# Last-slot products in pairs on half the rows, the last silu one round earlier, and sums stored by partition, in the tail of an attention and expert block

## The chip, the cores and the metric

The kernel runs on one core of a Trainium2 chip. The metric is the device time of one execution in microseconds (us). Engines are named as in the profile: PE is TensorE (PEld its weight loads), DVE VectorE, ACT ScalarE, POOL GpSimd, SP SyncE; SPq and ACTq are the DMAs that SP and ACT issue.

## What is computed

The input is x of 16 x 256 x 256 in float32. Two steps follow each other, each with its residual:

```
x = x + layernorm(attention(layernorm(x)))      # 16 heads of 128, weights as codes times scales
x = x + layernorm(ffn(layernorm(x)))

# ffn, tokens T = 4096, width 256, experts E = 64, K = 6 per token, capacity C = 96
pos  = sum(cumsum(onehot) * onehot) - 1          # place of a token in its expert's list
slot = expert * C + min(pos, C - 1)              # all that come too late share the last slot
out  = (silu(buf @ Wg.T) * (buf @ Wu.T)) @ Wd.T  # buf: the token in each slot
y    = sum over k of out[slot[t, k]] * weight[t, k]
ffn  = y + (silu(x @ Sg.T) * (x @ Su.T)) @ Sd.T  # one shared expert for all tokens
```

Each expert's last slot can serve many tokens, so its result has to be added to every token that overflowed, with that token's weight.

## The kernel before

The tokens are 32 chunks of 128 (NC = 32, P = 128), in 8 groups of 4 chunks (CG = 4). The first stage is attention and the routing. The second, `ffn`, is what the change is about, with some lines in the first that prepare for it.

**Experts.** The loop of L958 goes over 64 experts, 96 slots each. Each result is scaled by its token's weight (L909) and added by an indirect DMA of POOL (L910) to one of three arrays in HBM, `y_ds[0..2]` (from expert 44 on only the first two), at the row that the token's number says. That number travels with the token: `toki` (L127), copied into the row of `h` (L457), comes out as `toks` (L866). Three arrays are used so that an addition has not to wait for the one just before it. They are cleared in the first stage (`clear_sums`, L250), and for groups 0 to 3 the shared expert's result is what `y_ds[0]` begins with (`shared_put`, L770, L780). Row t of these arrays belongs to token t. The result of each expert's last slot is collected, row by row, into `ol`, of 64 x 256 (L917).

**Overflow.** In routing, each token's weights for last slots are set out as a 64 x 4096 array in HBM, `ovT_d` (L616). A group of tokens gets its last-slot contributions as a product of 64 rows: `ovT` of 64 x 128 (one chunk) times `ol` of 64 x 256.

**The tail.** The end of `ffn` (L997 to L1101) works through the 8 groups in the order `ends = [0, 5, 1, 2, 6, 3, 4, 7]` (L921). All of it is inside `tc.manual_schedule()`, so each engine runs its instructions in the order in which the code issues them. A round n, with g = ends[n], has these steps:

- `put_out(n, c)` (L997), for c = 0 and c = 2: PE makes the last-slot products of two chunks into one PSUM tile, ahead of them, for groups 5, 6 and 7, the last product of the shared expert (`shared_out`, L761, three products of up to 128 rows per chunk). The tile of c = 0 is from pool `ps`, that of c = 2 from `pso`; each pool has two buffers, so that round n can't begin to write before round n - 2 has been read. DVE adds the tile to the group's sum (L1008).
- `shared_in(*pieces[n])` (L1073): PE begins the shared expert's gate and up products for a later group, one third of its width at a time.
- `norm(n - 1, ...)` (L1035): DVE takes a reciprocal and a product (L1039, L1041), POOL another (L1042), and ACT scales the four chunks of the group before (L1045).
- `sum_y(n + 1)` (L1010): POOL adds up the sums that were loaded from HBM.
- POOL issues the addition of group n - 1 into the output, which holds the residual (L1082).
- DVE's two adds; `take_stats` (L1016): for some rounds another addition (L1021), then mean and variance of four chunks.
- `shared_act(*act)` (L1090): ACT's silu and DVE's product for the piece that the round before began.
- `take_root` (L1029): ACT's square root, L1032.

The last round leaves this loop at L1085 and does its adds, statistics and roots for two halves of the group, c = 0 and 2 (L1093), then the factors, the scaling and the residual (from `xl`) for both halves, and writes each half out by SP (L1101). Of the shared pieces, `pieces` (L922) says in which round each begins: (7, 2), the last one, in round 4, and so its silu comes in round 5:

```
if act:
    shared_act(*act)
act = pieces.get(n)
take_root(n, 0, CG)
```

The sums of the tail are loaded by SP: `load_early` (L938) loads the third array's and the first six groups' `ovT` during the experts; `load_ov` and 16 `load_sum` (L1052, L1056) come after the experts.

Of the kernel before, what the change touches and what calls it, by code (L numbers as in the profile page):

```python
# [9 lines left out]
F32 = mybir.dt.float32  # L10
# [4 lines left out]
ALU = mybir.AluOpType  # L15
# [3 lines left out]
P = 128  # L19
B, S, D = 16, 256, 256  # L20
NH, HD = 16, 128
FEAT = NH * HD
T = B * S
NC = T // P
# [4 lines left out]
E, M, CAP, K = 64, 176, 96, 6  # L29
# [7 lines left out]
CG = 4  # L37
# [6 lines left out]
SG0 = NC // CG // 2  # L44
# [6 lines left out]
def block_kernel(ctx, tc, x, wq, sq, wk, sk, wv, sv, wo, so, bqk, bv, bo, gateT, wg, wu, wd, sgT, suT, sdT, out):  # L51
    nc = tc.nc
    x_v = x.rearrange("(c p) d -> p c d", p=P)
    out_v = out.rearrange("(c p) d -> p c d", p=P)
# [4 lines left out]
    ovT_d = dram.tile([E, T], F32, name="ovT_d")  # L59
    buf_d = dram.tile([E * CAP, RW], F32, name="buf_d")  # L60

    y_ds = [dram.tile([T, D], F32, name=f"y{i}_d") for i in range(NY)]

    keep = ctx.enter_context(tc.tile_pool(name="keep", bufs=1))
    lastt = keep.tile([P, E], F32, name="lastt")
# [31 lines left out]
    def attention(split):  # L97
# [25 lines left out]
        base = rc.tile([P, E], F32, name="base")  # L123
        nc.gpsimd.iota(base, [[CAP, E]], base=1, channel_multiplier=0, allow_small_or_imprecise_dtypes=True)
        tokid = rc.tile([P, NC], F32, name="tokid")
        nc.gpsimd.iota(tokid, [[P, NC]], base=0, channel_multiplier=1, allow_small_or_imprecise_dtypes=True)
        toki = rc.tile([P, NC], I32, name="toki")  # L127
        nc.gpsimd.iota(toki, [[P, NC]], base=0, channel_multiplier=1)
        far = rc.tile([P, 1], F32, name="far")
        nc.gpsimd.iota(far, [[0, 1]], base=8192, channel_multiplier=8192, allow_small_or_imprecise_dtypes=True)  # L130
        nc.vector.memset(lastt, 0.0)
# [14 lines left out]
        zero = cp.tile([P, 256], F32, name="zero")  # L146
# [103 lines left out]
        def clear_sums(i):  # L250
            with tc.issue_after(marks[-1].ins):
                nc.vector.memset(zero, 0.0)
            r0 = 0 if i else SG0 * CG * P
            n = (T - r0) // P
            nc.sync.dma_start(
                y_ds[i][r0:T].rearrange("(p r) d -> p r d", p=P), zero.unsqueeze(1).to_broadcast([P, n, D])
            )

        in_mv = cp.tile([P, NC, 2], F32, name="in_mv")
        in_rs = cp.tile([P, NC], F32, name="in_rs")  # L260
# [398 lines left out]
        n = len(steps)  # L659
# [51 lines left out]
    def ffn(nm_, last_route, ph0):  # L711
# [10 lines left out]
        last = cp.tile([CAP, 1], F32, name="last")  # L722
        nc.gpsimd.iota(last, [[0, 1]], base=0, channel_multiplier=1, allow_small_or_imprecise_dtypes=True)
        nc.vector.tensor_scalar(last, last, float(CAP - 1), None, ALU.is_equal)
        ol = cp.tile([E, D], F32, name="ol")

        sg_t = cp.tile([P, DC, MS], F32, name="sg_t")
        nc.sync.dma_start(sg_t, sgT.rearrange("(c p) m -> p c m", p=P))
# [23 lines left out]
        def shared_act(g, i):  # L752
            m = MS_CH[i][1]
            if i == 0:
                aTs[g] = ep.tile([P, len(MS_CH), CG * P], F32, tag="aT", name=f"aT{g}")
            pg, pu = gus.pop((g, i))
            sg = ep.tile([P, CG * P], F32, tag="ssg", name=f"ssg{g}_{i}")
            nc.scalar.activation(sg[0:m, :], pg[0:m, :], AF.Silu)
            nc.vector.tensor_mul(aTs[g][0:m, i, :], sg[0:m, :], pu[0:m, :])

        def shared_out(po, g, c, start, stop):  # L761
            for i, (m0, m) in enumerate(MS_CH):
                nc.tensor.matmul(
                    po, lhsT=aTs[g][0:m, i, c * P : (c + 1) * P], rhs=sd_t[0:m, i, :],
                    start=start and i == 0, stop=stop and i == len(MS_CH) - 1,
                )
# [3 lines left out]
        def shared_put(g, c):  # L770

            if c == 0:
                ss[g] = ep.tile([P, CG, D], F32, tag="ssg2", name=f"s{g}", bufs=1)
            s = ss[g]
            po = ps.tile([P, 2, D], F32, tag="o", name=f"so{g}_{c}")
            for i in range(2):
                shared_out(po[:, i, :], g, c + i, True, True)
            nc.scalar.copy(s[:, c : c + 2, :], po)
            if c and g < SG0:
                nc.scalar.dma_start(y_ds[0][g * CG * P : (g + 1) * CG * P].rearrange("(c p) d -> p c d", p=P), s)  # L780

        NG_ = E // EG
        wts, bns, bTs, wcs, toks, prods, acts, obs = {}, {}, {}, {}, {}, {}, {}, {}
# [137 lines left out]
        ends = [0, G, 1, 2, G + 1, 3, SG0, G + 2]  # L921
        pieces = {0: (G + 1, 1), 1: (G + 1, 2), 2: (G + 2, 0), 3: (G + 2, 1), 4: (G + 2, 2)}  # L922
        direct = (1, 3, 5)
        ys, ovTs, stat = {}, {}, {}
        Y, V = CG * D, CG * P

        def place(t, at, g, i):

            ys.setdefault(g, {})[i] = t[:, at : at + Y].rearrange("p (c d) -> p c d", d=D)

        def load_sum(g, i):
            nc.sync.dma_start(ys[g][i], y_ds[i][g * V : (g + 1) * V].rearrange("(c p) d -> p c d", p=P))

        def load_ov(t, at, g):
            ovTs[g] = t[0:E, at : at + V]
            nc.sync.dma_start(ovTs[g], ovT_d[:, g * V : (g + 1) * V])

        def load_early(k):  # L938

# [9 lines left out]
        with tc.manual_schedule():  # L949
# [8 lines left out]
            for e in range(E + 2):  # L958
                g, j = e // EG, e % EG
# [23 lines left out]
                g, j = divmod(e - 1, EG)  # L983
# [10 lines left out]
            yp = ph5.enter_context(tc.tile_pool(name="yp" + nm_, bufs=2, reuse_waits="tile"))  # L994
            pso = ph7.enter_context(tc.tile_pool(name="pso" + nm_, bufs=2, side="right", space=PSUM, reuse_waits="tile"))

            def put_out(n, c):  # L997

                g = ends[n]
                y = ys[g][0 if n in direct else 2][:, c : c + 2, :]  # L1000
                po = (pso if c else ps).tile([P, 2, D], F32, tag="o", name=f"ov{g}_{c}")
                for i in range(2):
                    if g > SG0:
                        shared_out(po[:, i, :], g, c + i, True, False)
                    nc.tensor.matmul(
                        po[:, i, :], lhsT=ovTs[g][:, (c + i) * P : (c + i + 1) * P], rhs=ol, start=g <= SG0, stop=True
                    )
                return lambda: nc.vector.tensor_tensor(y, y, po, ALU.add)  # L1008

            def sum_y(n):  # L1010
                y = ys[ends[n]]
# [17 lines left out]
            def take_root(n, c, m):  # L1029
                g = ends[n]  # L1030
                rs = yp.tile([P, m], F32, tag=f"rs{m}", name=f"rs{g}_{c}")
                nc.scalar.activation(rs, stat[g, c][:, :, 1], AF.Sqrt, bias=eps_t)  # L1032
                stat[g, c] = rs, stat[g, c]

            def norm(n, c, m, eng):  # L1035

                g = ends[n]
                rs, mv = stat.pop((g, c))
                nc.vector.reciprocal(rs, rs)  # L1039
                nb = yp.tile([P, m], F32, tag=f"nb{m}", name=f"nb{g}_{c}")  # L1040
                nc.vector.tensor_scalar(nb, rs, -1.0, None, ALU.mult)  # L1041
                eng.tensor_tensor(nb, nb, mv[:, :, 0], ALU.mult)  # L1042
                y = ys[g][0]
                for i in range(m):
                    nc.scalar.activation(  # L1045
                        y[:, c + i, :], y[:, c + i, :], AF.Identity, bias=nb[:, i : i + 1], scale=rs[:, i : i + 1]
                    )

            nt, last = len(ends), ends[-1]
            t = xp.tile([P, EG * RW], F32, tag="bn", name="yv", bufs=5)  # L1050
            for i, g in enumerate(ends[EWB:]):
                load_ov(t, i * V, g)  # L1052
            nc.gpsimd.tensor_add(ys[SG0][2], ys[SG0][2], ss[SG0])
            for g in ends:
                for i in range(2):
# [2 lines left out]
            t = xp.tile([P, EG * RW], F32, tag="bn", name="xl", bufs=5)  # L1058
            xl = t[:, 0:Y].rearrange("p (c d) -> p c d", d=D)
# [8 lines left out]
            sum_y(0)  # L1068
            act = (G + 1, 0)
            for n, g in enumerate(ends):  # L1070
                add = [put_out(n, 0), put_out(n, 2)]
                if n in pieces:
                    shared_in(*pieces[n])  # L1073

                if n:
                    norm(n - 1, 0, CG, nc.gpsimd)
                if n + 1 < nt:
                    sum_y(n + 1)
                if n:
                    h = ends[n - 1]  # L1080
                    behind_stored(
                        nc.gpsimd.dma_start(out_v[:, h * CG : (h + 1) * CG, :], ys[h][0], accum_op=ALU.add), h  # L1082
                    )
                if n + 1 == nt:
                    break  # L1085
                for f in add:
                    f()
                take_stats(n, 0, CG)
                if act:
                    shared_act(*act)  # L1090
                act = pieces.get(n)
                take_root(n, 0, CG)
            for f, c in zip(add, (0, 2)):  # L1093
                f()
                take_stats(n, c, 2)
                take_root(n, c, 2)
            for c, eng in ((0, nc.gpsimd), (2, nc.vector)):
                norm(n, c, 2, eng)
                y = ys[last][0][:, c : c + 2, :]
                eng.tensor_add(y, y, xl[:, c : c + 2, :])  # L1100
                nc.sync.dma_start(out_v[:, last * CG + c : last * CG + c + 2, :], y)  # L1101
            ph7.close()
            ph5.close()
            ph4.close()
# [3 lines left out]
    flag, r, ph0 = attention(True)  # L1108
# [46 lines left out]
```

## Time and profile before

| | us |
|---|---|
| median of 3 runs | 1474.4 (1471.49 to 1476.71) |
| the profiled execution, its own time | 1477.35 |
| its span in the profile | 1475.5 |
| PE busy | 1428.8 (97%) |
| DVE busy | 1108.1 (75%) |
| ACT busy | 670.8 (45%) |
| POOL busy | 370.2 (25%) |

The span is that of the records of one execution on the chip; the execution's own time is 1.85 us more. A row of the profile names the source line, the engine, the operation, what is written from what, and the tile's partitions x elements. Products of float32 are recorded as two PE records each. "Idle before" is the time for which the engine stood, and the arrow names what released it. A table by windows gives busy time and, in brackets, the number of instructions of each engine in a stretch of time, then the TensorE clock that was granted (1.00 is full), the mean busy share of the DMA engines, and GB/s.

### The profile page before, as it was taken

The numbers are of one execution on the slowest core, as the hardware profiler recorded it, in microseconds if no ns is written. First come the engines' busy times: TensorE is split into PE (matmuls) and PEld (weight loads), VectorE is DVE, ScalarE is ACT, GpSimd is POOL, SyncE is SP. The second block draws the span as 40 slices with busy tenths as digits, with TensorE's granted clock in tenths as the row PEclk, the third lists the DMA queues.
The fourth block names the chain that finished last, engine by engine and source line by source line (L and its number), as shares of the span: only waits on it lengthen the run. The fifth ranks groups of instructions, "written<-read, shape, count | busy, mean of one in ns | idle before, by whom it ended". The sixth has DMA issues, their size and how long they took to land. (4 is left out here: it accounts for less than half of the span.)

```text
span 1475.5 us, 24749 instructions
## 1 busy us (share of the span) xinstructions
PE 1428.8 (97%) x8476; PEld 1208.6 (82%) x8476; DVE 1108.1 (75%) x3489; ACT 670.8 (45%) x1800; POOL 370.2 (25%) x345
## 2 busy tenths in 40 slices
PE   7999999999999999999999999999999999999995
PEld 4689899898989898898989898988798568878653
DVE  5787898878898988989798989888987324434364
ACT  4553463445444545544454445455454322323253
POOL 2330000230041006001400420060243315544572
PEclk9899999999999999999999999999999999999996
DMA  5246140240011101101010001001013979999594
GB/s 169 74 128 182 58 143 16 76 138 30 1 43 34 44 16 32 44 30 28 25 54 15 26 29 51 8 9 38 12 54 96 284 206 225 258 254 226 106 248 70
DMA packets 102928, 132.08 MB, mean 90 GB/s; under 512 B 15290, under 2 KB 85216, under 8 KB 102266
## 3 DMA queue, kind: packets, MB, share of 16 engines
q1 hardware_dynamic: 70570, 93.44, 21.2%
q0 software_dynamic: 21872, 20.75, 7.2%
q10 hardware_dynamic: 10352, 16.22, 3.8%
q8 instruction: 70, 1.15, 0.3%
q14 instruction: 64, 0.52, 0.1%
HBM read 82.50 MB, written 70.19 MB: 103 GB/s over the span
## 5 line engine op out<-in xcount | busy, mean ns | idle before, releaser
L336 ACT ACTIVATE pe<-sc,nms 128x256 f32<-128x256 f32 x512 | 240.2, 475 | 207.1 <-DVE nms L332 144.4
L594 POOL DMA_INDIRECT buf_d<-h,si x192 | 189.7, 988 | 508.5 <-DVE si L591 430.0
L361 PE MATMUL po<-pT,v 128*128 128x256 f32 x1024 | 277.0, 383 | 3.3 <-DVE oT L365 2.1
L328 PE MATMUL sc<-qk 128*128 128x256 f32 x1024 | 268.3, 382 | 1.4 <-ACT pT L352 0.7
L352 ACT COPY pT<-pt 128x512 f32<-128x512 f32 x256 | 150.4, 587 | 217.9 <-PE pt L350 217.1
L316 PE MATMUL pq<-xnT,wq 128*128 128x256 f32 x1024 | 216.2, 326 | 0.6 <-DVE wq L200 0.4
L361 PEld LDWEIGHTS po<-pT,v 128*128 128x128 f32 x1024 | 176.2, 191 | 23.5 <-ACT pT L352 3.5
L328 PEld LDWEIGHTS sc<-qk 128*128 128x128 f32 x1024 | 175.5, 190 | 18.5 <-issue 2.5
L321 DVE TENSOR_TENSOR qk<-pq,bqk_t 128x512 f32<-128x512 f32 x256 | 174.8, 683 | 13.4 <-PE pq L316 12.1
L330 DVE TENSOR_REDUCE nm<-sc 128x2 f32<-128x512 f32 x256 | 174.8, 683 | 12.9 <-PE sc L328 10.4
L350 PE MATMUL pt<-ident,pe 128*128 128x128 f32 x1024 | 172.0, 278 | 2.1 <-DVE pe L342 1.0
L316 PE MATMUL pq<-xnT,wk 128*128 128x256 f32 x1024 | 172.1, 287 | 0.4 <-DVE wk L200 0.4
L342 DVE TENSOR_SCALAR pe<-pe,rsum 128x256 f32<-128x256 f32 x512 | 168.4, 371 | 1.2
L316 PEld LDWEIGHTS pq<-xnT,wq 128*128 128x128 f32 x1024 | 157.1, 191 | 14.7 <-issue 1.5
L301 PE MATMUL pv<-wv,xnT 128*128 128x512 f32 x512 | 162.8, 439 | 2.7 <-POOL wv L204 2.6
L350 PEld LDWEIGHTS pt<-ident,pe 128*128 128x128 f32 x1024 | 125.7, 141 | 45.7 <-issue 8.4
L363 DVE TENSOR_SCALAR oT<-po,bv_t 128x256 fp32r<-128x256 f32 x256 | 122.7, 479 | 52.2 <-PE po L361 50.1
L316 PEld LDWEIGHTS pq<-xnT,wk 128*128 128x128 f32 x1024 | 141.8, 190 | 2.5 <-DVE wk L200 1.1
L380 PE MATMUL pp<-wo,oT 128*128 128x256 f32 x1024 | 132.5, 286 | 0.0
L380 PEld LDWEIGHTS pp<-wo,oT 128*128 128x128 f32 x1024 | 125.1, 189 | 0.8
L365 DVE SCALAR_TENSOR_TENSOR oT<-po,bv_t,oT 128x256 fp32r<-128x256 f32 x256 | 122.0, 477 | 2.7
L910 POOL DMA_INDIRECT y_d<-ob,tok x64 | 91.3, 1427 | 110.7 <-DMA y_d<-ob,tok 26.0
(211 smaller groups left out, 1808.2 us busy)
## 6 DMA issues: line engine op xcount, KB each, us to landing
y<-y_d SPq DMA_DIRECT2D x24, 512.0 KB
y_d<-zero SPq DMA_DIRECT2D x2, 4096.0 KB
w<-wg SPq DMA_DIRECT2D x40, 176.0 KB
w<-wu SPq DMA_DIRECT2D x40, 176.0 KB
w<-wd SPq DMA_DIRECT2D x40, 176.0 KB
buf_d<-empty SPq DMA_DIRECT2D x1, 6528.0 KB
bn<-buf_d ACTq DMA_DIRECT2D x11, 408.0 KB
w<-wg SPq DMA_DIRECT2D x6, 704.0 KB
```

Of the source, the lines that this page charges most:

```text
L301: nc.tensor.matmul(pv, lhsT=x[:, dc, c * P : (c + 1) * P], rhs=ws["wv", j][:, dc, :], start=i == 0, stop=i == len(terms) - 1,)
L316: nc.tensor.matmul(pq[:, m, :], lhsT=w[:, dc, o : o + HD], rhs=x[:, dc, :], start=i == 0, stop=i == len(terms) - 1,)
L321: marks[0:] = [nc.vector.tensor_tensor(qk, pq, bqk_t[:, h, :].unsqueeze(2).to_broadcast([P, 2, S]), ALU.add)]
L328: nc.tensor.matmul(sc[:, c, :], lhsT=qk[:, 0, c * P : (c + 1) * P], rhs=qk[:, 1, :], start=True, stop=True)
L330: nc.vector.tensor_reduce(nm, sc, AX.X, ALU.max, negate=True)
L336: nc.scalar.activation(pe[:, c, :], sc[:, c, :], AF.Exp, bias=nms[:, c : c + 1], scale=SC, accum_out=ssum[:, c : c + 1])
L342: nc.vector.tensor_scalar_mul(pe[:, c, :], pe[:, c, :], rs[:, c : c + 1])
L350: nc.tensor.transpose(pt[:, kc, c * P : (c + 1) * P], pe[:, c, kc * P : (kc + 1) * P], ident)
L352: nc.scalar.copy(pT[b, h], pt)
L361: nc.tensor.matmul(po, lhsT=v[:, kc, o : o + HD], rhs=t[:, kc, :], start=kc == 0, stop=kc == 1)
L380: nc.tensor.matmul(pp, lhsT=x[:, h, c * P : (c + 1) * P], rhs=ws["wo", h // HPG][:, h % HPG, :], start=i == 0, stop=i == len(terms) - 1,)
L594: ins = nc.gpsimd.indirect_dma_start(out=buf_d[:, :], out_offset=bass.IndirectOffsetOnAxis(ap=si[:, c, k : k + 1], axis=0), in_=h[:, c, :] ...
```

## The change

Four things change.

- **Pairs.** The last-slot weights of a group are kept as two halves: chunks 0 and 1 on partitions 0 to 63, chunks 2 and 3 on partitions 64 to 127. `load_ov` makes two transfers of half the size. `ol` gets 128 partitions, and SP copies its first 64 into the others after the last `load_ov`. `put_out` now makes the products of both PSUM tiles in one call: for i = 0 and 1, the shared products of chunk i and chunk 2 + i, and then their two last-slot products, one on rows 0 to 63 and one on rows 64 to 127 of the array.
- **The last silu.** In round 4 (`max(pieces)`) `shared_act` is called for the piece that this very round began, so that round 5 has none.
- **The last group by chunks.** The half of chunks 0 and 1 goes through factors, scaling, residual and output before the second half's add is issued. Its factors are now all on DVE. In the second half chunk 2 is scaled on ACT and chunk 3 on DVE; DVE adds the residual to chunk 3 and then to chunk 2, and each goes out in its own transfer, on ACT's and SP's queues.
- **Numbering.** Row p * 32 + c of the sums now belongs to partition p of chunk c. `toki`, the clearing, `shared_put` and `load_sum` follow, so that a group's sums are 4 KB in one piece for each partition, instead of four pieces of 1 KB. The addition's DMAs are as before but for the rows that they name.

```diff
+    def sum_rows(i, c0, c1):
+        return y_ds[i].rearrange("(p c) d -> p c d", p=P)[:, c0:c1, :]
...
-        nc.gpsimd.iota(toki, [[P, NC]], base=0, channel_multiplier=1)
+        nc.gpsimd.iota(toki, [[1, NC]], base=0, channel_multiplier=NC)
...
-            r0 = 0 if i else SG0 * CG * P
-            n = (T - r0) // P
-            nc.sync.dma_start(
-                y_ds[i][r0:T].rearrange("(p r) d -> p r d", p=P), zero.unsqueeze(1).to_broadcast([P, n, D])
-            )
+            c0 = 0 if i else SG0 * CG
+            nc.sync.dma_start(sum_rows(i, c0, NC), zero.unsqueeze(1).to_broadcast([P, NC - c0, D]))
...
-        ol = cp.tile([E, D], F32, name="ol")
+        ol = cp.tile([P, D], F32, name="ol")
...
-                nc.scalar.dma_start(y_ds[0][g * CG * P : (g + 1) * CG * P].rearrange("(c p) d -> p c d", p=P), s)
+                nc.scalar.dma_start(sum_rows(0, g * CG, (g + 1) * CG), s)
...
-            nc.sync.dma_start(ys[g][i], y_ds[i][g * V : (g + 1) * V].rearrange("(c p) d -> p c d", p=P))
+            nc.sync.dma_start(ys[g][i], sum_rows(i, g * CG, (g + 1) * CG))
...
-            ovTs[g] = t[0:E, at : at + V]
-            nc.sync.dma_start(ovTs[g], ovT_d[:, g * V : (g + 1) * V])
+            ovTs[g] = t[:, at : at + H]
+            for i in range(2):
+                nc.sync.dma_start(ovTs[g][i * E : (i + 1) * E], ovT_d[:, g * V + i * H : g * V + (i + 1) * H])
...
-            def put_out(n, c):
+            def put_out(n):
                 g = ends[n]
-                y = ys[g][0 if n in direct else 2][:, c : c + 2, :]
-                po = (pso if c else ps).tile([P, 2, D], F32, tag="o", name=f"ov{g}_{c}")
+                po = [p_.tile([P, 2, D], F32, tag="o", name=f"ov{g}_{i}") for i, p_ in enumerate((ps, pso))]
                 for i in range(2):
                     if g > SG0:
-                        shared_out(po[:, i, :], g, c + i, True, False)
-                    nc.tensor.matmul(
-                        po[:, i, :], lhsT=ovTs[g][:, (c + i) * P : (c + i + 1) * P], rhs=ol, start=g <= SG0, stop=True
-                    )
-                return lambda: nc.vector.tensor_tensor(y, y, po, ALU.add)
+                        for c in range(2):
+                            shared_out(po[c][:, i, :], g, 2 * c + i, True, False)
+                    for c in range(2):
+                        rows = slice(c * E, (c + 1) * E)
+                        nc.tensor.matmul(
+                            po[c][:, i, :], lhsT=ovTs[g][rows, i * P : (i + 1) * P], rhs=ol[rows], start=g <= SG0, stop=True
+                        )
+                def add(c):
+                    y = ys[g][0 if n in direct else 2][:, 2 * c : 2 * c + 2, :]
+                    return lambda: nc.vector.tensor_tensor(y, y, po[c], ALU.add)
+                return [add(c) for c in range(2)]
...
-                load_ov(t, i * V, g)
+                load_ov(t, i * H, g)
+            nc.sync.dma_start(ol[E:P], ol[0:E])
...
                 act = pieces.get(n)
+                if n == max(pieces):
+                    shared_act(*act)
+                    act = None
                 take_root(n, 0, CG)
+
+            y = ys[last][0]
+            outs = (nc.sync, nc.scalar)
             for f, c in zip(add, (0, 2)):
                 f()
                 take_stats(n, c, 2)
                 take_root(n, c, 2)
-            for c, eng in ((0, nc.gpsimd), (2, nc.vector)):
-                norm(n, c, 2, eng)
-                y = ys[last][0][:, c : c + 2, :]
-                eng.tensor_add(y, y, xl[:, c : c + 2, :])
-                nc.sync.dma_start(out_v[:, last * CG + c : last * CG + c + 2, :], y)
+                rs, nb = factors(n, c, 2, nc.vector)
+                if c == 0:
+                    scale(y, 0, 2, rs, nb)
+                    nc.gpsimd.tensor_add(y[:, 0:2, :], y[:, 0:2, :], xl[:, 0:2, :])
+                    nc.sync.dma_start(out_v[:, last * CG : last * CG + 2, :], y[:, 0:2, :])
+                    continue
+                scale(y, 2, 1, rs, nb)
+                nc.vector.tensor_scalar(y[:, 3, :], y[:, 3, :], rs[:, 1:2], nb[:, 1:2], ALU.mult, ALU.add)
+                for i in (3, 2):
+                    nc.vector.tensor_add(y[:, i, :], y[:, i, :], xl[:, i, :])
+                    outs[i % 2].dma_start(out_v[:, last * CG + i, :], y[:, i, :])
```

`factors` and `scale` are the two parts of `norm`; elsewhere they are called one after the other as before.

More of the change, by code (lines that the diff above doesn't have):

```diff
@@ L925, in ffn @@
         Y, V = CG * D, CG * P
+        H = V // 2
         def place(t, at, g, i):
@@ L1033, in take_root, with factors @@
                 stat[g, c] = rs, stat[g, c]
-            def norm(n, c, m, eng):
+            def factors(n, c, m, eng):
                 g = ends[n]
@@ L1042, in norm, with scale @@
                 eng.tensor_tensor(nb, nb, mv[:, :, 0], ALU.mult)
-                y = ys[g][0]
+                return rs, nb
+            def scale(y, c, m, rs, nb):
                 for i in range(m):
@@ L1070, in ffn @@
             for n, g in enumerate(ends):
-                add = [put_out(n, 0), put_out(n, 2)]
+                add = put_out(n)
                 if n in pieces:
@@ L1075, in ffn @@
                 if n:
-                    norm(n - 1, 0, CG, nc.gpsimd)
+                    scale(ys[ends[n - 1]][0], 0, CG, *factors(n - 1, 0, CG, nc.gpsimd))
                 if n + 1 < nt:
```

## The prediction, made before any run of the changed kernel

> **What bounds the kernel now.** I read the page first: TensorE (PE) is busy 97% of the span, and its clock row falls only in the last slice. The page's own chain of waits reaches back just to 1463.95 us, so I took the tables of busy time by window, and then the timeline of the last 100 us engine by engine. Windows (PE, weight loads, DVE, ACT, POOL, clock, DMA):
>
> ```profile
> 1430.00:1440.00 10.00, 10.00 (x34) 5.58 (x34) 5.51 (x14) 4.66 (x7) 6.08 (x4) 1.00 0.58 80
> 1440.00:1450.00 10.00, 6.86 (x22) 4.37 (x21) 6.85 (x18) 8.47 (x14) 6.09 (x5) 0.81 0.45 62
> 1450.00:1460.00 10.00, 10.00 (x21) 5.85 (x21) 6.13 (x17) 2.68 (x7) 2.99 (x4) 0.50 0.53 64
> ```
>
> PE does 34 products in 10 us at clock 1.00, then 21 at 0.50. The timeline shows why (start, duration, engine, line; in brackets the idle time before and its releaser):
>
> ```profile
> 1434.96 0.69 DVE L1008 TENSOR_TENSOR y<-y,ov 128x512 f32<-128x512 f32 x1 [3.55 <-PE ov L1005]
> ...
> 1441.22 1.29 DVE L1008 TENSOR_TENSOR y<-y,ov 128x512 f32<-128x512 f32 x2
> ...
> 1443.71 1.28 ACT L758 ACT_TABLE_LOAD   x1
> ...
> 1445.01 0.59 ACT L758 ACTIVATE ssg<-sp 96x512 f32<-96x512 f32 x1
> 1445.62 1.28 ACT L1032 ACT_TABLE_LOAD   x1
> 1445.63 0.68 DVE L759 TENSOR_TENSOR aT<-ssg,sp 96x512 f32<-96x512 f32 x1 [1.00 <-ACT ssg L758]
> 1446.37 0.50 PEld L763 LDWEIGHTS ov<-sd_t,aT 96*128 96x128 f32 x2 [3.54 <-DVE aT L759]
> 1446.37 1.22 PE L763 MATMUL ov<-sd_t,aT 96*128 96x256 f32 x2 [3.14 <-DVE aT L759]
> ...
> 1447.54 1.28 DVE L1008 TENSOR_TENSOR y<-y,ov 128x512 f32<-128x512 f32 x2
> ...
> 1454.27 0.69 DVE L1008 TENSOR_TENSOR y<-y,ov 128x512 f32<-128x512 f32 x1
> ...
> 1460.80 0.69 DVE L1008 TENSOR_TENSOR y<-y,ov 128x512 f32<-128x512 f32 x1 [3.83 <-PE ov L1005]
> ```
>
> Call the eight rounds 0 to 7; round n's adds are the L1008 rows. Round 4 waits for PE (3.55 us). From there the loop add, statistics, root, factors, add sets the pace; its step from round 5 to 6 holds two table loads around the last silu. Meanwhile PE stands 3.14 us for that silu's product, falls to half clock, and so round 7's second half comes 3.83 us late.
>
> The cost of a 64-row product is read here:
>
> ```profile
> 1403.49 1.46 PE L763 MATMUL ov<-sd_t,aT 128*128 128x256 f32 x6
> 1404.88 0.70 PE L1005 MATMUL ov<-ol,y 64*128 64x256 f32 x2
> 1405.50 1.56 PE L763 MATMUL ov<-sd_t,aT 128*128 128x256 f32 x6
> 1407.00 0.70 PE L1005 MATMUL ov<-ol,y 64*128 64x256 f32 x2
> ```
>
> An f32 product is two records. Weight loads inside one shape follow at 0.214 us, so six take 1.28 and two 0.43. From 1404.88 to 1407.00 is 2.12: 0.41 more than eight records (1.71). That is what one excursion from 128 rows to 64 and back costs. Eight records in one excursion (1398.03 to 1399.95) take 1.92, of which 0.21 is over inside and the rest at its edges.
>
> **Part 1, products in pairs.** Rounds 0, 2, 3 have 8 records on 64 rows; rounds 1, 4, 7 have four excursions each, which become two, so 2 x 0.42 = 0.84 us is saved in each whatever the pairs do. No row shows products on both halves at once. Bounds: no overlap saves 0; full overlap halves the records. The Trainium skill, "TensorE: Matmul & The Clock Gate", Part 3 (Packing small matmuls), says products on different row groups run together, a pack taking one product and about 4 ns per further tile: 0.43 per pair. But the same section says products start in order. Each here is two records one after the other on one half, so in A1 A2 B1 B2 only A2 and B1 can meet: three steps instead of four for a pair, five instead of eight for two pairs in a row. I take that, since the rows do stand in this order. By the page's full overlap the whole sum would be 11.2 instead of 10.2. Ahead of round 4's add it saves 3 x 3 x 0.214 = 1.93 (rounds 0, 2, 3), 2 x 2 x 0.214 = 0.86 (rounds 1, 4) and 1.68 of excursions: 4.47 us. PE would finish round 4 at 1434.9 - 4.5 = 1430.4. DVE's factors of round 3 end at 1430.3 today, so DVE can follow. But both halves now come at PE's end; before, the first add (0.69) lay beside PE. **A: 4.5 - 0.7 = 3.8 us.** With no overlap it is 1.0; with full overlap DVE and ACT bind first, at about 4.8.
>
> Its operands: eight more loads of half size. SP stands 16.7 and 15.3 us for buffers in the early ones; the last two add 1.35 to the 1.35 from 1386.66. Then the new copy of ol makes SP wait for the last ol row (issued at 1386.62 on ACT's queue). Behind it stand the 16 loads of sums, but their first waits for a scatter until 1393.42 anyway. With the shortest landing of a scatter (3.2 us) for each hop, the copy is there near 1394; round 0's products start at 1398.03. Zero, with 4 us to spare; beyond that PE stands for the excess.
>
> **Part 2, the silu moved up.** In round 4 ACT gets a second silu (0.6) after PE's last shared_in (3.6 us after round 4's products, so 1434.0), ended by 1434.8; round 4's statistics end near 1435.4. DVE's second product (0.68) lies beside the table load (1.28) that the root needs anyway. Zero from add 4 to add 5 (5.57 us today). If the silu came later than the statistics, its 0.6 would be on the path. In round 5 both table loads and the silu leave: today the statistics end at 1444.64 and the root starts at 1446.91; now it can start at 1444.67. **B: 2.2 us.** From add 6 to add 7 nothing changes (6.73 us, with one DVE add slowed to 2.39 beside POOL).
>
> PE's stall does not vanish. Round 7's products need the PSUM buffers of round 5's adds. PE comes there at 1434.0 + 2 x 1.07 + 0.42 = 1436.5 and add 5 frees the first buffer at 1441.22 - 3.8 + 0.7 = 1438.1, so it stands some 1.6 us, on PSUM instead of the silu. Then 30 records and two excursions, 30 x 0.214 + 0.84 = 7.2 us at full clock, give 1445.3, against add 7 at 1454.27 - 3.8 - 2.2 = 1448.2: hidden, 2.9 to spare.
>
> Would 1.6 us halve the clock? The same page, Part 1 (The HAM clock gate), says half clock follows an idle window of about 3.4 us, so 1.6 would do nothing. This trace says less:
>
> ```profile
> 1246.59 0.34 PE L897 MATMUL ap<-ident,prod 96*88 96x96 f32 x2 [2.14 <-DVE eq L856]
> ...
> 1185.35 1.96 PE L747 MATMUL sp<-hs,sg_t 128*128 128x512 f32 x4 [2.19 <-DMA hs<-hT_d]
> ...
> 1248.00:1249.00 1.00, 1.00 (x6) 0.98 (x5) 0.38 (x2) 0.30 (x1) 0.13 (x1) 0.66 1.18 350
> 1249.00:1250.00 1.00, 1.00 (x6) 0.88 (x5) 0.00 (x0) 0.07 (x1) 0.61 (x1) 0.50 1.07 268
> ```
>
> 2.14 us of idling brought 3.4 us at 0.50, while 2.19 us at 1185 left the clock at 1.00. So it can go either way. By the rule nothing is lost and the sum stays 10.2; by the worse row, with half clock to the end as today (14.4 us from 1446.37), round 7's products end at 1452.5, 4.3 late, and the sum is 5.9. I take 0, as 1.6 is below both rows.
>
> **Part 3, last group by chunks.** Today, from add 7 (1454.27) to the end of the last DVE add (1467.01) is 12.74 us. After: first statistics end at +2.7; root and factors, now ahead of the second add on DVE, take 0.9 (1463.45 to 1464.34 today): +3.6. Second add to statistics 2.6 (1460.80 to 1463.41): +6.2. Root and factors 0.9: +7.1. One chunk scaled on ACT (0.52) beside one on DVE (0.37, as L342), then two adds of half the 0.93 row: +8.5. **C: 12.7 - 8.5 = 4.2 us**, 3.8 of it the vanished PE wait. POOL's add and the first output lie beside the second half. Two last transfers of 128 KB instead of one of 256: zero to 0.4 gained; I take zero.
>
> **Part 4, numbering.** The iota is one instruction as before; sums move in 4 KB pieces instead of 1 KB. Sixteen loads take 21.9 us for 8.4 MB, so 383 GB/s already. PE does not wait for them: zero, gain at most some 1 us where POOL waits (5.4 us for the first). The scatters write rows 32 KB apart instead of 1 KB; no row shows that.
>
> **Sum:** 3.8 + 2.2 + 4.2 = 10.2 us. The profiled execution (1477.35, span 1475.5) would be 1467.1; it is 3 us above the median, so the median 1474.4 becomes 1464.2.
>
> **Rivals.** (1) Pairs do not overlap: A is 1.0, the sum 7.4, time 1467.0. For it: no row shows overlap; against it: the order leaves A2 and B1 free to meet. (2) PE's new stall halves the clock: up to 4.3 back, time 1466.5 to 1468.5. For it the row at 1246.59. Both together, or a stretch of DVE waiting for POOL, leave about 3.5: 1471, which is no difference. (3) Slower: the scatters to rows 32 KB apart. At the end one is due each 2.4 us, the time of an expert, on two buffers in turn, so each may take 4.8 us; today one takes 3.3 (1390.16, until the first load of sums at 1393.42) to 5.3 (1382.69, until the next on its buffer at 1387.97). At 6.3 us the last seven on a buffer fall 7 x 1.5 = 10 us behind, the sums come 10 us late, round 0's DVE and POOL work with them, and the gain is gone: that is the point. At 8 us they are 22 late: 1486. Against it: 1 KB rows at scattered tokens already.
>
> **Chances.** Forecast 0.50 (1461.5 to 1466), no overlap 0.18, half clock 0.16, both or a new wait 0.12, slower 0.04. A measurement can tell about 0.3% (4.4 us) from no change: faster 0.84, same 0.12, slower 0.04. The range 1460.5 to 1470 takes in full overlap (1.0 less), the loads' bound (1.0) and 1.7 of the runs' own spread (5.2 over three) below, and most of the rivals above.
>
> **What would show it.** Right: round 1's and round 4's adds in one piece; starts of B1 within A2's duration; no table load after round 4; clock 1.00 through round 7; last DVE add 8.5 us after add 7. Wrong: four even steps of 0.214 in a pair; clock 0.50 after 1438; DVE waiting for PE in round 7; scatters above 4.8 us.

## The result, and the profile after

The median went from 1472.95 us (4 runs, 1471.25 to 1476.71) to 1458.55 us (4 runs, 1456.67 to 1461.23): a ratio of 0.990, 95% interval 0.9874 to 0.9927, or 14.4 us less. The forecast was 1464.2 and its range began at 1460.5, so the direction was right and the gain 4 us larger than the sum said. The changed kernel in a later group of runs (`e11_change_again`) gave 1461.2 us and 0.9919 (0.9893 to 0.9945). In the runs e1 to e8 every kernel, the one before too, takes some 180 to 190 us longer (before: 1651.5 us beside e1 to e4, 1665.5 beside e5 to e8), lost in eight stretches of the attention stage, so their times are compared only with those of before beside them.

The profiled execution of after took 1458.62 us, with a span of 1456.7. Its windows answer to the first three lines of the prediction (start and end, length, then PE, weight loads, DVE, ACT, POOL, clock, DMA share, GB/s):

```profile
1420.00:1430.00 10.00, 8.40 (x39) 4.63 (x38) 7.97 (x20) 7.88 (x14) 8.36 (x6) 1.00 0.45 59
1430.00:1440.00 10.00, 6.11 (x30) 4.25 (x28) 8.69 (x24) 3.80 (x9) 6.43 (x6) 1.00 0.96 131
1440.00:1450.00 10.00, 0.00 (x0) 0.00 (x0) 6.57 (x21) 4.15 (x9) 2.55 (x2) 0.51 0.67 127
```

PE ends its last product in the second window, at clock 1.00; the clock falls only when PE has nothing left to do. From 1430 on DVE is the busiest engine. The timeline of after, same columns as in the prediction (L1012 is the last-slot product, L1018 its add, L1044 the root, L1127 the last residual):

```profile
1421.35 0.70 PE L1012 MATMUL ov<-ol,y 64*128 64x256 f32 x4
...
1422.08 1.28 DVE L1018 TENSOR_TENSOR y<-y,ov 128x512 f32<-128x512 f32 x2 [0.95 <-PE ov L1012]
...
1425.93 1.28 ACT L1044 ACT_TABLE_LOAD   x1
...
1428.44 1.28 DVE L1018 TENSOR_TENSOR y<-y,ov 128x512 f32<-128x512 f32 x2
...
1429.19 2.86 PE L764 MATMUL ov<-sd_t,aT 128*128 128x256 f32 x12 [1.60 <-DVE y L1018]
...
1432.58 1.28 DVE L1018 TENSOR_TENSOR y<-y,ov 128x512 f32<-128x512 f32 x2
...
1439.32 0.69 DVE L1018 TENSOR_TENSOR y<-y,ov 128x512 f32<-128x512 f32 x1
...
1447.08 0.76 DVE L1127 TENSOR_TENSOR y<-y,xl 128x256 f32<-128x256 f32 x2
```

Rounds 4, 5, 6 and 7 are the four L1018 rows. Round 4's add is in one piece and still waits for PE, by 0.95 us. ACT's last table load stands before round 5's add. PE's 3.14 us wait for the silu has become one of 1.60 us for DVE's read of the PSUM. Round 7 no longer waits for PE.

I split the two spans at two marks that both traces have: the shared expert's first product and round 0's first last-slot product. From the second mark to the end of the span I call it the tail. A column is the time from one event to the next; "add n" means the adds of round n, "last add" is the last residual.

| us | before | after | gain | forecast |
|---|---|---|---|---|
| span | 1475.5 | 1456.7 | 18.8 | 10.2 |
| of it: to the first shared product | 1135.89 | 1131.61 | 4.3 | 0 |
| first shared product to expert 0 | 70.47 | 68.03 | 2.4 | 0 |
| expert 0 to round 0 | 191.67 | 191.35 | 0.3 | 0 |
| tail: round 0 to end of add 4 | 37.62 | 32.38 | 5.24 | 3.8 |
| end of add 4 to start of add 5 | 5.57 | 5.08 | 0.49 | 0 |
| add 5 to add 6 | 6.32 | 4.13 | 2.19 | 2.2 |
| add 6 to add 7 | 6.73 | 6.74 | 0.0 | 0 |
| add 7 to end of last add | 12.74 | 8.52 | 4.22 | 4.2 |
| last add to end of span | 8.46 | 8.89 | -0.43 | 0 |

The tail's rows sum to 11.7. The first 4.3 us are no gain of the change. They are a fall of the TensorE clock in the attention stage, from 60.5 to 70.7 us, that the profile of before happens to have and the first profile of after has not. Three windows of one stretch, the first of before, the second of after, the third of the changed kernel run again:

```profile
60.00:65.00 5.00, 5.00 (x15) 3.23 (x15) 2.32 (x8) 2.19 (x6) 1.27 (x1) 0.55 0.34 104
```

```profile
60.00:65.00 5.00, 4.70 (x24) 3.45 (x24) 3.51 (x10) 3.22 (x9) 2.03 (x3) 1.00 0.37 111
```

```profile
60.00:65.00 5.00, 4.84 (x15) 3.12 (x15) 2.64 (x9) 2.19 (x6) 1.38 (x2) 0.60 0.36 110
```

At clock 0.55 and 0.60 PE does 15 products in 5 us, at 1.00 it does 24. The same kernel shows both: its first shared product comes at 1131.61 us in one profile and at 1135.82 in the other, as in before. That would also account for the 4.4 us by which the profile of before (1477.35) lies above the median of its runs. Without it 14.5 us are left, which is what the medians say. What has to be explained is 2.4 us at the shared expert and 11.7 us in the tail.

### The profile page after: what moved, and what is told of

It is laid out like the page before. It is cut to its first block, busy times and chain, and to the rows that moved or that the text cites. A ratio compares the mean times of both kernels' runs of the same rounds, so it can differ in the third digit from the quotient of the medians.

```text
span 1456.7 us, 24761 instructions
## 1 busy us (share of the span) xinstructions
PE 1407.3 (97%) x8476; PEld 1197.6 (82%) x8476; DVE 1109.4 (76%) x3492; ACT 666.4 (46%) x1797; POOL 371.3 (25%) x344
## 5 line engine op out<-in xcount | busy, mean ns | idle before, releaser
L322 DVE TENSOR_TENSOR qk<-pq,bqk_t 128x512 f32<-128x512 f32 x256 | 174.6, 682 | 12.1 <-PE pq L317 10.7
L331 DVE TENSOR_REDUCE nm<-sc 128x2 f32<-128x512 f32 x256 | 174.6, 682 | 11.7 <-PE sc L329 9.2
L317 PEld LDWEIGHTS pq<-xnT,wq 128*128 128x128 f32 x1024 | 156.6, 191 | 14.5 <-issue 1.5
```

The lines of the kernel that those rows point to most:

```text
L317: nc.tensor.matmul(pq[:, m, :], lhsT=w[:, dc, o : o + HD], rhs=x[:, dc, :], start=i == 0, stop=i == len(terms) - 1,)
L322: marks[0:] = [nc.vector.tensor_tensor(qk, pq, bqk_t[:, h, :].unsqueeze(2).to_broadcast([P, 2, S]), ALU.add)]
L331: nc.vector.tensor_reduce(nm, sc, AX.X, ALU.max, negate=True)
```

## The experiments

The theory to be tested: the two halves overlap more than I took, the silu's table loads give what was forecast, and the last 4 us come from PE not being late, whatever the order of the last group. Its rivals are named in each expectation. In e1 to e8 single runs of one kernel lie up to 14 us from their median, and the changed kernel itself was not timed beside them. The totals of e1 to e4, 1638.6 to 1641.1 us, cannot be told apart, though their tails differ by 4 us. So the argument rests on the segments of the profiles, one profile for each kernel, and the totals come second. The table has the segments of all of them, in us; "base" is the kernel that was edited.

| kernel | base | to end of add 4 | 4 to 5 | 5 to 6 | 6 to 7 | 7 to last add | to end | tail |
|---|---|---|---|---|---|---|---|---|
| before | | 37.62 | 5.57 | 6.32 | 6.73 | 12.74 | 8.46 | 77.44 |
| after | | 32.38 | 5.08 | 4.13 | 6.74 | 8.52 | 8.89 | 65.75 |
| e1 old numbering | after | 33.29 | 5.13 | 4.14 | 6.75 | 8.53 | 8.91 | 66.75 |
| e2 one half | after | 36.23 | 5.02 | 4.13 | 6.74 | 8.52 | 8.91 | 69.54 |
| e3 silu late | after | 32.69 | 5.76 | 6.32 | 7.95 | 8.32 | 7.76 | 68.79 |
| e4 old last group | after | 32.38 | 5.08 | 4.13 | 6.74 | 8.78 | 8.44 | 65.56 |
| e5 numbering alone | before | 37.62 | 5.57 | 6.32 | 6.74 | 10.30 | 8.32 | 74.87 |
| e6 silu alone | before | 37.62 | 4.94 | 4.13 | 6.74 | 8.79 | 8.43 | 70.65 |
| e7 pairs alone | before | 32.38 | 5.69 | 6.32 | 6.78 | 8.79 | 8.45 | 68.40 |
| e8 stores on SP | before | 37.62 | 5.57 | 6.32 | 6.73 | 12.75 | 8.32 | 77.32 |
| e9 halves in turn | after | 32.62 | 5.14 | 4.13 | 6.74 | 8.52 | 8.85 | 66.0 |
| e10 six direct | after | 32.38 | 5.07 | 5.14 | 4.14 | 8.80 | 9.53 | 65.06 |
| e11 change again | after | 32.38 | 5.08 | 4.14 | 6.75 | 8.53 | 8.79 | 65.66 |

### Undoing one part: e1 to e4

**Old numbering.**

```diff
-        return y_ds[i].rearrange("(p c) d -> p c d", p=P)[:, c0:c1, :]
+        return y_ds[i].rearrange("(c p) d -> p c d", p=P)[:, c0:c1, :]
...
-        nc.gpsimd.iota(toki, [[1, NC]], base=0, channel_multiplier=NC)
+        nc.gpsimd.iota(toki, [[P, NC]], base=0, channel_multiplier=1)
```

(and the clearing as before.)

> The changed kernel with rows of the sums numbered by token again; the rest of the change stays. Theory: the new numbering is worth 2.4 us before the tail, because the stores of the shared sums go out in 128 pieces of 4 KB instead of 512 of 1 KB, and the load of a group's hidden rows behind them on ACT's queue arrives in time. So about 1461 us, PE waits some 2 us for hs again near 1180 us, and the tail from round 0's products to the end stays near 66 us. Rival, the prediction's account: numbering is worth nothing and the 2.4 us is chance: 1458.6 us, no wait for hs.

Measured: 1638.59 us, ratio to before 0.9922 (0.9893 to 0.995); tail 66.75. The 16 loads of sums are issued in 20.9 us, from the first to the last; in after it is 16.4. Its adds of rounds 2 and 3 come 0.6 and 1.0 us later than in after. But e7, which has the old numbering too, reaches the end of add 4 at 32.38 like after. So the slower loads cost up to 1.0 us in the tail, and in one kernel of two. The other place is before the experts: PE waits 1.82 us for `hs` again, as before (2.19).

**All last-slot products on rows 0 to 63**, in the new order.

```diff
-            ovTs[g] = t[:, at : at + H]
-            for i in range(2):
-                nc.sync.dma_start(ovTs[g][i * E : (i + 1) * E], ovT_d[:, g * V + i * H : g * V + (i + 1) * H])
+            ovTs[g] = t[0:E, at : at + V]
+            nc.sync.dma_start(ovTs[g], ovT_d[:, g * V : (g + 1) * V])
...
-                            po[c][:, i, :], lhsT=ovTs[g][rows, i * P : (i + 1) * P], rhs=ol[rows], start=g <= SG0, stop=True
+                            po[c][:, i, :], lhsT=ovTs[g][:, k * P : (k + 1) * P], rhs=ol[0:E], start=g <= SG0, stop=True
```

(with k = 2c + i, and without the copy of `ol`.)

> The changed kernel with all last-slot products on rows 0 to 63, in the same order, so that the two of a pair cannot overlap; the excursions into 64 rows stay as few. Theory (pairs overlap fully): rounds 0, 2, 3 lose 4 records each and rounds 1, 4 lose 4 each, 20 x 0.214 = 4.3 us, all on the path to round 4's add: about 1462.9 us. Rival, the prediction's account (three steps of four, so 13 records): 2.8 us, 1461.4. If DVE and ACT bound the rounds up to 4, less than 1 us.

Measured: 1640.03 us, 0.9936 (0.9915 to 0.9958); tail 69.54, end of add 4 at 36.23, 3.85 later than after. The row of the eight records of round 0, here in e2, then in after:

```profile
1566.95 1.99 PE L1011 MATMUL ov<-ol,y 64*128 64x256 f32 x8
```

```profile
1390.99 1.13 PE L1012 MATMUL ov<-ol,y 64*128 64x256 f32 x8
```

1.99 to 1.13 is 0.86, which is four steps of 0.215 out of eight. The two halves overlap in full. In after the eight starts are 1390.988, 1390.994, 1391.308, 1391.314, 1391.524, 1391.530, 1391.739 and 1391.746: four pairs, 6 ns inside a pair.

**The last silu in round 5 again.**

```diff
-                if n == max(pieces):
-                    shared_act(*act)
-                    act = None
```

> The changed kernel with the last silu back in round 5. Theory (what the move is worth is mostly the clock): PE stands some 5 to 6 us for the silu's product, falls to half clock, and round 7's products end some 4.5 us after DVE could take them: together 7 us, about 1465.5 us, clock 0.50 at the end. Rival (only the two table loads count): 2.5 us, about 1461, clock 1.00 through round 7.

Measured: 1640.04 us, 0.9941 (0.9923 to 0.9958); tail 68.79, 3.0 more than after. Add 5 to 6 is 6.32 as before, with both table loads. PE stands 2.29 and then 2.82 us and falls to half clock, but for 10.2 us only. Round 7's add is 1.2 us late for that, not 4. So it lies near the smaller of the sizes, for a mixed reason: 2.9 us of table loads, 1.2 of PE, less 1.1 at the end.

**The old end of the last group.**

```diff
-                rs, nb = factors(n, c, 2, nc.vector)
-                if c == 0:
-                    scale(y, 0, 2, rs, nb)
...
+            for c, eng in ((0, nc.gpsimd), (2, nc.vector)):
+                y = ys[last][0]
+                scale(y, c, 2, *factors(n, c, 2, eng))
+                y = y[:, c : c + 2, :]
+                eng.tensor_add(y, y, xl[:, c : c + 2, :])
+                nc.sync.dma_start(out_v[:, last * CG + c : last * CG + c + 2, :], y)
```

> The changed kernel with the last group finished as before (both roots first, both halves scaled on ACT, two outputs of 256 KB). Theory: the 4.2 us from the last round's first add to the last add came from PE no longer being late (3.8); the new order by chunks is worth 0.4: about 1459 us, 8.9 us from first add to last add. Rival: the order by chunks carries the 4.2 us itself: 1462.8.

Measured: 1641.12 us, 0.9936 (0.9918 to 0.9955); tail 65.56, 0.2 less than after. The last add comes 0.26 us later, the end of the span 0.45 us sooner after it. The new order of the last group is worth nothing that shows, and 4.0 of the 4.2 us between add 7 and the last add are there without it.

### One part alone: e5 to e7

**Numbering alone**, on the kernel before.

```diff
-        nc.gpsimd.iota(toki, [[P, NC]], base=0, channel_multiplier=1)
+        nc.gpsimd.iota(toki, [[1, NC]], base=0, channel_multiplier=NC)
...
-                nc.scalar.dma_start(y_ds[0][g * CG * P : (g + 1) * CG * P].rearrange("(c p) d -> p c d", p=P), s)
+                nc.scalar.dma_start(sum_rows(0, g * CG, (g + 1) * CG), s)
...
-            nc.sync.dma_start(ys[g][i], y_ds[i][g * V : (g + 1) * V].rearrange("(c p) d -> p c d", p=P))
+            nc.sync.dma_start(ys[g][i], sum_rows(i, g * CG, (g + 1) * CG))
```

(and the clearing.)

> The kernel before with the new numbering alone. Theory: 2.4 us less, about 1470.5 us, no PE wait for hs near 1185 us, tail unchanged near 77.5 us from round 0's products to the end. Rival, numbering is worth nothing: 1473 us, the wait stays.

Measured: 1665.31 us, 0.9998 (0.9983 to 1.0013), nothing that a timing shows; tail 74.87, 2.6 less than before. The tail's gain is chance: with the same 3.14 us stall of PE the clock was at half for 10.2 us here (1635.6 to 1645.9), and to the end in the profile of before. Up to add 7 every segment is that of before. Ahead of the tail, PE's wait for `hs` is 1.45 us.

**The silu alone**, on the kernel before.

```diff
+                if n == max(pieces):
+                    shared_act(*act)
+                    act = None
```

> The kernel before with the last silu moved up alone. Theory: PE no longer stands 3 us for the silu's product and stays at full clock; round 7's products are done near 1451, DVE's add 7 comes at 1452 and the last add 8.9 us later, 6.1 us less than before: about 1466.9 us, clock 1.00 to the end. Rival, only the table loads count: 2.2 us, 1470.8.

Measured: 1662.83 us, 0.9977 (0.9963 to 0.9991); tail 70.65, 6.8 less. Beside the 2.2 us of table loads and 0.6 ahead of add 5, it takes PE's lateness away. PE's last products and the two adds of round 7 in e6:

```profile
1644.30 0.70 PE L1005 MATMUL ov<-ol,yv 64*128 64x256 f32 x2
1645.81 0.69 DVE L1008 TENSOR_TENSOR y<-y,ov 128x512 f32<-128x512 f32 x1
...
1648.41 0.65 DVE L1008 TENSOR_TENSOR y<-y,ov 128x512 f32<-128x512 f32 x1
```

PE ends 0.8 us before the first add; the second does not wait. In before it waited 3.83. PE has no stall for the silu here, and its clock is at 1.00 until its last product.

**The pairs alone**: the kernel of e1 with the old end of the last group (the edit of e4), and without the silu's move.

```diff
-                if n == max(pieces):
-                    shared_act(*act)
-                    act = None
```

> The kernel before with the pairs alone. Theory: round 4's adds end 5.2 us earlier, but PE then stands longer for the last silu and does round 7 at half clock, so some 4.2 us remain: about 1468.8 us, clock 0.50 in round 7. Rival: all 5.2 us come through and more, if the clock stays: 1466 or less.

Measured: 1660.89 us, 0.9965 (0.9952 to 0.9978); tail 68.40, 9.0 less, where I had expected 4.2. PE still stands for the silu and still falls to half clock, but its last product ends just in time. In e7:

```profile
1631.66 3.78 PE L767 MATMUL ov<-sd_t,aT 96*128 96x256 f32 x8 [3.28 <-DVE aT L763]
...
1638.87 0.70 PE L1015 MATMUL ov<-ol,yv 64*128 64x256 f32 x4
1639.60 0.69 DVE L1021 TENSOR_TENSOR y<-y,ov 128x512 f32<-128x512 f32 x1
```

That is a shorter fall of the clock, and not shown to be the pairs. From the end of the stall to PE's last product, in before, then in e7 (the clock is the third number from the end):

```profile
1446.37:1460.76 14.39, 14.39 (x28) 8.04 (x28) 8.76 (x21) 5.57 (x12) 5.28 (x5) 0.50 0.65 86
```

```profile
1631.66:1639.57 7.91, 7.91 (x28) 5.39 (x28) 6.28 (x15) 3.20 (x7) 3.79 (x3) 0.75 0.67 87
```

PE is busy throughout. At half clock it spent 14.4 us in before and 3.9 in e7 (9.0 in e5). An estimate from these two lines: with only 3.9 us at half clock PE would have ended 5.2 us sooner in before, which is more than the 3.83 us that DVE waited; with half clock throughout it would have ended 4.0 us later in e7. So the clock's history alone can make either order late or punctual. e3, which has the pairs and the late silu too, was 1.2 us late.

The silu's move is another matter. In all eight profiles that have it (after, e1, e2, e4, e6, e9, e10, e11) the clock stays at 1.00 until PE's last product; in all five without it (before, e3, e5, e7, e8) it falls. The 4 us behind add 7 can be gained only once: 9.0 + 6.8 = 15.8 alone, but 10.7 in e1, which has both. The totals of e6 and e7, 2.7 and 4.6 us below before, are smaller than their tails say by some 4 us each. Part of it may be the clock, since the tail of before is 77.4 us with its long fall and 74.9 with e5's; which of the two the timed runs had is not known, and I leave it open.

### The wait for hs: e8

**The stores of the shared expert's sums on SP's queue**, on the kernel before.

```diff
-                nc.scalar.dma_start(y_ds[0][g * CG * P : (g + 1) * CG * P].rearrange("(c p) d -> p c d", p=P), s)
+                nc.sync.dma_start(y_ds[0][g * CG * P : (g + 1) * CG * P].rearrange("(c p) d -> p c d", p=P), s)
```

> The kernel before with the four stores of shared sums issued by SP instead of ACT; pieces of 1 KB as before. Theory A (the load of hs stands behind the store in ACT's queue): the PE wait for hs goes, 2.4 us less, 1470.5 us. Theory B (the number of pieces loads all DMA engines, whatever the queue): the wait stays or moves to the weights, 1473 us.

Measured: 1676.75 us, 1.0063 (1.0038 to 1.0088), 10.5 us slower by that ratio, which neither theory had forecast; from the first shared product to expert 0 82.1 us instead of 70.5. ACT's copy into `s`, which has one buffer, waits for the store before it. From e8, ACT and PE:

```profile
1374.66 0.58 ACT L778 COPY s<-so 128x512 f32<-128x512 f32 x1 [16.57 <-DMA y_d<-s]
...
1376.29 3.43 PE L747 MATMUL sp<-hs,sg_t 128*128 128x512 f32 x4 [5.06 <-ACT ssg L758]
```

So the landing of this store does set PE's time in this stage. It lands later here because SP issues it later: 8.9 us after the copy that fills `s`, where ACT did so after 0.03 in before. From its issue to ACT's next copy it is 14.4 us, against 17.0. What e8 does not tell is why the store takes longer under the old numbering.

### How far the halves overlap, and one step on: e9 to e11

**Two products on one half, then two on the other** (for groups 0 to 4).

```diff
+                        for i in range(2):
+                            nc.tensor.matmul(
+                                po[c][:, i, :], lhsT=ovTs[g][rows, i * P : (i + 1) * P], rhs=ol[rows], start=True, stop=True
+                            )
```

(inside the loop over c, instead of c inside i.)

> The changed kernel with the four products of the groups without shared products issued half by half: two on rows 0 to 63, then two on rows 64 to 127. Theory A (PE keeps the order of issue, so only neighbours meet): 8 records take 7 steps of 0.214 instead of 4, 0.64 us more in rounds 0, 2 and 3, tail 1.9 us longer. Theory B (the two halves run as queues of their own, whatever the order): tail as in the changed kernel, 65.7 us.

Measured: 1462.14 us, 0.9914 (0.989 to 0.9939); tail 66.0. Round 0's eight records in e9:

```profile
1394.77 1.14 PE L1020 MATMUL ov<-ol,y 64*128 64x256 f32 x8
```

1.14 us as in after, in four pairs 13 to 15 ns apart, though the four records of one half are issued before the first of the other. The order of issue inside this group does not limit the overlap.

**Round 6's third sum added by POOL** (on e4).

```diff
-        direct = (1, 3, 5)
+        direct = (1, 3, 5, 6)
```

> The changed kernel with the old end of the last group, and with the third sum of round 6's group added by POOL instead of DVE. Theory: the DVE addition of 2.4 us, slowed by POOL, leaves the path from add 6 to add 7, and POOL's longer round 5 gives 0.9 back: tail 64.1 us, from 65.6. Rival: POOL becomes the bound of rounds 6 and 7, tail 66 or more.

Measured: 1460.37 us, 0.9904 (0.9877 to 0.993), against 1461.2 for e11 on the same chip: no difference that can be measured. Add 6 to 7 falls from 6.74 to 4.14; add 5 to 6 grows by 1.0 and the last stretch by 1.1 over e4. The tail is 65.06, 0.5 less than e4, where 1.5 less was expected; POOL did not become the bound.

**The changed kernel again.** No edit.

> The changed kernel itself, beside the others on one chip. Theory: round 0 to the end 65.7 us as in its first profile (77.4 before), the store of shared sums off ACT's path (third copy of s 41.3 us after the first shared product), and 13 to 15 us less than before. Rival: part of the 14.4 us was the two kernels' luck with the clock in the first stage: 11 to 12 us less.

Measured: 1461.2 us, 0.9919 (0.9893 to 0.9945); tail 65.66. The tail repeats to 0.1 us; the fall of the clock at 60 us was shown above.

## Why the prediction was right or wrong

**Pairs: right in kind, too small.** The step that failed is "three steps of four for a pair, five instead of eight for two pairs in a row. I take that, since the rows do stand in this order". I had put the page's start in order against the page's full overlap and taken the former; full overlap came (1.13 us for eight records, and e9). With it the prediction's sum is 3 x 4 x 0.214 + 4 x 2 x 0.214 + 1.68 = 5.96, less 0.7 for the add: 5.3, against 5.24 measured. "With full overlap DVE and ACT bind first, at about 4.8" failed as well: DVE still stood 0.95 us for PE at add 4. That excursions alone give 1.0 (rival 1) was about right: e2, which has only them, gained 1.4. The Trainium skill, "TensorE: Matmul & The Clock Gate", Part 3 (Packing small matmuls), has both rules: a pack takes one product and about 4 ns per further tile, and products start in order. Here the first holds (starts 6 ns apart inside a pair), and the second put no limit on it (e9).

**Operands of the pairs: right.** Round 0's first weight load stands 0.76 us in after, by the trace for its own issue and not for a DMA.

**The silu: right.** Add 5 to 6 fell by 2.19 (forecast 2.2). Add 4 to 5, forecast at zero, gave 0.49: the root's table load (1425.93) now follows the silu at once instead of waiting for the statistics, which end at 1427.1. PE's new stall was 1.60 us (forecast 1.6) and left the clock at 1.00.

**The last group: right size, but not by its order.** 8.52 us were forecast and measured, and the prediction did say of its 4.2 us that 3.8 were "the vanished PE wait". It booked them under the last group and did not ask which part makes the wait vanish. With the old order and PE punctual, the same stretch is 8.78 (e4; 8.79 in e6 and e7). So 4.0 us belong to PE being punctual and 0.26 to the order. The silu's move alone brings it about (e6). For the pairs alone it is not shown, since e7 owes it to the clock. From the last add to the end the prediction put "zero to 0.4 gained"; it was 0.43 lost (8.46 to 8.89). That the two smaller transfers cost this is not shown: the same stretch is 7.76 us in e3, with two transfers, and 9.53 in e10, with one.

**The numbering: the step that failed is "PE does not wait for them: zero".** It covers the loads of the sums alone. These are 4 us faster (16.4 us for 16, 20.5 before) and hidden, as said, but for the 0.9 us that e1 lost without them up to the end of add 4. The store of the shared expert's sums has the same pieces, and there PE does wait. ACT's rows in before, then in after:

```profile
1163.25 0.38 ACTq L780 DMA_DIRECT2D y_d<-s  x1
...
1180.21 1.07 ACT L778 COPY s<-so 128x512 f32<-128x512 f32 x2 [10.20 <-DMA y_d<-s]
```

```profile
1158.96 0.33 ACTq L781 DMA_DIRECT2D y_d<-s  x1
...
1172.87 0.58 ACT L779 COPY s<-so 128x512 f32<-128x512 f32 x1 [7.15 <-PE so L764]
```

In before the copy starts 17.0 us after the store's issue, held by the store; in after 13.9 us, held by PE. From the first shared product to this copy it is 41.27 us in all eight kernels with the new numbering (after, e2 to e5, e9 to e11) and 44.1 to 44.5 in all four with the old one that leave the store on ACT's queue (before, e1, e6, e7). The load of `hs` on the same queue behind the store then lets PE wait 1.82 to 2.35 us in those four, and at most 1.45 in the eight. That the numbering causes this is shown. That it is the larger pieces, and not the places in HBM, is argued, since no run changed one without the other. From the first shared product to expert 0 the four profiles of after, e9, e10 and e11 all take 68.0 us, before 70.5; on the chips of e1 to e8 the gain is smaller, 68.7 to 69.8 us (e2 to e5) against 70.1 to 70.6 (e1, e6, e7). In a timed run it does not stand out: e5's ratio is 0.9998 (0.9983 to 1.0013). So 2.4 us are what the two traces differ by, and the timed worth lies between none and about 2.8.

**Rivals.** The clock did not fall (rival 2), in none of the eight profiles with the silu moved up. The rows that the prediction weighed did not make that certain: in before the clock also fell at 60.5 us, after pauses of 0.97 and 0.55 us only, and the prediction left that row out. The scatters were no slower (rival 3): expert 0 to round 0 takes 191.35 us, 191.67 before. How little that says is seen from the same kernel again, 188.8 us in e11; a smaller cost of the scatters would not show.

**The sum.** 10.2 + 1.44 (pairs) + 0.49 (add 4 to 5) + 2.44 (wait for `hs`) - 0.43 (end) = 14.1; from the median of the first three runs, 1474.4, that gives 1460.3, and from that of all four, 1472.95, 1458.8. The range failed because its lower end had only 1.0 for the pairs and 1.0 for all DMA effects of the numbering, and 1.45 us of the miss are the fourth run of before, which moved its median. That the sum meets the measured time so closely is in part luck: 4.2 us of it are read from a profile of before in which the clock stayed at half to the end, and with e5's clock they would be 1.8.

## What to carry to other kernels

When an engine arrives late at the end of a tail, book that lateness once, by itself, and ask of each part whether it alone removes it: here the silu's move did, while the lateness was booked under another part. Before a part alone is credited, compare the clock over the same work: a shorter fall did in e7 what the pairs seemed to do. When a layout in HBM changes, list every DMA that uses it, stores too, with what is queued behind it and which single buffer it holds: the loads that the prediction named were hidden, and the store that it did not name held up PE. And before a fall of the clock is booked as cost or gain, look whether the same kernel shows it in a second profile.

## What the runs showed of the hardware that was not expected

- Products of 64 rows on the two halves run side by side even if one half's are all issued first: four records per half in 1.14 us (e9), 1.99 on one half (e2).
- How long the clock stays at half varies for one and the same stall, with PE busy all the while. With PE's 3.14 us stall it was 10.2 us in e5 and up to PE's end in before and e8 (over 14.4 us); it was 6.8 us in e7 with 3.28, and 10.2 us in e3 after 2.29. The Trainium skill, "TensorE: Matmul & The Clock Gate", Part 1 (The HAM clock gate), names an idle window of about 3.4 us; here pauses of 0.97 and 0.55 us close together at 58 us went ahead of 10.2 us of half clock in before, the same two (0.95 and 0.55) of none in after, and 1.60 us (after, 1429) did nothing.
- The same store was issued 0.03 us after its copy by ACT (before) and 8.9 us after it by SP (e8), and was followed by ACT's next copy 17.0 and 14.4 us after its issue. The late issue, not a slower transfer, is what e8 paid for.
